# Two graph-attention and feed-forward layers on one core: the third attention's value stride, the experts' order on VectorE, and when the feed-forward stage loads its last rows

## Chip, cores and metric

The kernel runs as one program on one core of a Trainium2 chip. Its engines are TensorE (PE in the profile; PEld is its weight load), VectorE (DVE), ScalarE (ACT), GpSimd (POOL) and SyncE (SP), which here only issues DMAs. Each engine works through its own list of instructions in order, and waits on semaphores for the others.

The metric is the device time of one execution in microseconds. Before the change it is 2967.96 us (median of 3 runs, 2966.99 to 2968.54).

## What is computed

Input are 4096 rows `x` of 256 numbers and a 4096 x 4096 matrix `adj` of zeros and ones. Four blocks follow each other, each on the layer-normed result of the one before and added to it:

```python
x = x + L0_gnn(layernorm(x), adj)       # one graph attention, 4 heads of 64
x = x + L0_ffn(layernorm(x))            # 30 steps of a small recurrence
x = x + L1_gnn(layernorm(x), adj)       # two graph attentions, one after the other
x = x + L1_ffn(layernorm(x))            # a mixture of 6 experts, the best 2 for each row

# a graph attention, for each head:
h = x @ W;  f1 = h @ a1;  f2 = h @ a2
e = leaky_relu(f1[:, None] + f2[None, :], 0.2);  e = where(adj > 0, e, -9e15)
out = elu(softmax(e) @ h)

# a step of L0_ffn:
h = h + 0.01 * tanh(h);  h = h * sigmoid(h);  h = layernorm(h, ln_w, ln_b);  h = h @ W + b

# L1_ffn:
p = softmax(relu(f @ router_w1 + b1) @ router_w2 + b2);  top_w, top_i = top_k(p, 2)
r = softmax(top_w)
h1 = relu(f @ expert_w1 + b1);  h2 = relu(h1 @ expert_w2 + b2);  o = h2 @ expert_w3 + b3
y = sum over the two chosen experts of r * o
```

## The kernel before

The 4096 rows are 32 tiles of 128 rows (`NT`), or 8 groups of four tiles (`NG`, `G`). Intermediate rows go through tensors in device memory: `x1d` after the first attention, `x2d` after the feed-forward, `h1d` and `x3d` after the second and third attention. A ring of four row groups (`ring`, `load_ahead`) stays in SBUF all the time and is shared by all stages.

**Attention** (`attention`, called three times: tags g0, g1, g2). A front (L394 to L439) loads the row groups, turns them on TensorE, multiplies them with the weights, and makes for each tile and head the values `vals`: fp16, two parts of 2 x 65 numbers (upper and lower half of the number, and a column for the denominator). Then the main loop goes through 4 chunks of 8 tiles, 4 heads, and 8 steps of four tiles each (`units`, 128 in all). In a unit ScalarE and VectorE make the signs `st` (L464, L462), VectorE ands and xors them with the mask of edges (L569, L575), and TensorE does 64 matmuls (L521): an fp8 mask tile as weights, 130 columns of `vals` moving, accumulated in PSUM over all 32 source tiles. A head's sums are closed (`close`) by small VectorE and ScalarE operations between the next units. VectorE and ScalarE keep the written order in the main loop (`manual_schedule`); elsewhere a scheduler orders what engines and queues do.

The two numbers `apart` set how far the two parts of `vals` stand from each other in SBUF, in fp16 elements, and how far the two accumulators stand from each other in PSUM, in fp32 elements. The layers have (130, 130), (160, 130) and (130, 256): 260, 320 and 260 bytes for the values. The third layer has no layer norm ahead of it (`norm` is False); there, the sum over all rows that the front ends with goes through `xsb` (L431), a copy by GpSimd that spreads a column over 128 columns, which then are TensorE's weights in L435.

**Feed-forward** (L827 to L966). 30 steps for each of 8 row groups are 240 units; `slot(at)` is one turn of a pipeline over them, and holds pieces of six units: TensorE's turns of the rows `z` (L869, unit at-3), VectorE's `y` out of PSUM (L877, at-5), ScalarE's silu `z` and its fp16 half (L893, L897, at-2), VectorE's `lower` half (L898), a transposing DMA on SP (L902), ScalarE's tanh `th` (L907, unit at), GpSimd's sum of it (L908), VectorE's statistics (L917), ScalarE's `zT` (L924), GpSimd's power for the deviation (L928), and TensorE's product (L937, L940, at-4). PSUM holds two products `po`, so a unit's product waits for the `y` of the unit two before it. GpSimd's sum is made to follow `lower` by `follows`.

The stage's rows are the first attention's result, normed in place: `measure` (VectorE), `rate` (ScalarE and three GpSimd operations), `init` (ScalarE, or VectorE where `apart` is True). What is left of this when the attention ends is spread over the first slots by the table `opening`. The last step of the recurrence adds the same rows again. `slot` loads them a second time at slots 32, 56, ... 200 of the program's order (`load` for groups 0 to 3 into the ring, `load_apart` for the others); as SP is left to the scheduler, these eight loads can be issued as soon as their buffers are free.

**Experts** (from L1021). The rows are two halves of 2048 (`NTH` tiles and `NGH` groups each). `route(h)` norms a half, turns it (L1122), multiplies it with the router's weights (L1101, L1131), finds the best two experts of each row, and builds the list of rows by expert: `source` (which row is gathered into a place), `dest` (where its result goes), `expert` (which expert a tile of 128 places belongs to), `bsel` (that expert's biases), `ws` (the two weights). `route(0)` runs ahead, with the experts' weights `ew` loaded after its first four steps; `route(1)` is taken step by step in the loop over 74 tiles (`gather`, `turn`, `fetch`, `hidden`, `result`), where `fetch` reads the expert's number into registers. Each half's rows come through the ring, and ScalarE writes them, less one, to `acc`, to which `combine` adds the experts' results.

Of the kernel before, what the change touches and what calls it, by code (L numbers as in the profile page):

```python
# [23 lines left out]
P = 128  # L24
# [22 lines left out]
def gnn_ffn_kernel(ctx: ExitStack, tc: tile.TileContext, a: dict, out: bass.AP):  # L47
# [34 lines left out]
    def rows_of(t, g):  # L82
        return t[g * GR : (g + 1) * GR, :].rearrange("(r p) c -> p r c", p=P)
# [6 lines left out]
    def load_ahead(src, g, view=rows_of, queue=nc.sync):  # L90
        t = ring[:, turns[0] % 4]
        turns[0] += 1
        queue.dma_start(t, view(src, g))
        ahead[g] = t

    def over_std(pool, src):

        st = pool.tile([P, G, 6], F32, name="ln_st")
        mv = pool.tile([P, G, 2], F32, name="ln_mv")
        for r in range(G):  # L100
            nc.vector.bn_stats(st[:, r, :], src[:, r, :])  # L101
        for r in range(G):
            nc.vector.bn_aggr(mv[:, r, :], st[:, r, :])
        rstd = pool.tile([P, G], F32, name="ln_rstd")
        nc.vector.tensor_scalar(rstd, mv[:, :, 1], EPS, None, op0=OP.add)
        nc.gpsimd.tensor_tensor(rstd, rstd, mhalf, OP.pow)
        return rstd, mv
# [53 lines left out]
    def attention(tag, src, norm, w, front, chunks, first, ends, following, side={}, apart=(2 * DV, 2 * DV)):  # L161
# [7 lines left out]
        with ExitStack() as scope:  # L169
# [68 lines left out]
            with ExitStack() as ps:  # L238
# [189 lines left out]
                if sums is None:  # L428
                    xt = prep.tile([P, KC], F32, name="xt")
                    nc.vector.tensor_reduce(xt, xs, axis=AX.X, op=OP.add)  # L430
                    xsb = prep.tile([P, KC, P], F32, name="xsb")  # L431
                    nc.gpsimd.tensor_copy(xsb, xt[:, :, None].to_broadcast([P, KC, P]))
                    pt = small_ps()
                    for k in range(KC):
                        nc.tensor.matmul(pt[:, :C], xsb[:, k, :], w[:, k, :C], start=(k == 0), stop=(k == KC - 1))  # L435
                nc.scalar.activation(
# [304 lines left out]

    def load(g, queue=nc.sync):
        if g not in ahead:
            load_ahead(x1d, g, queue=queue)
        x1[g] = ahead.pop(g)

    def measure(g):
# [79 lines left out]
    with ExitStack() as scope:  # L827
# [7 lines left out]
        def load_apart(src, g):  # L835
            x1[g] = hold.tile([P, G, C], F32, name="x1")
            nc.sync.dma_start(x1[g], rows_of(src, g))

        for g in range(4, NG):
# [5 lines left out]

        th, zs, mvs, rs, zT, zT16, pos = {}, {}, {}, {}, {}, {}, {}
        units = FFN_STEPS * NG
        opening = {
            0: [(init, 2)],
            1: [(rate, 4), (rate, 5), (init, 3, True)],  # L850
            2: [(init, 4, True)],
            3: [(init, 5, True), (measure, 6)],
            4: [(rate, 6), (measure, 7)],
            5: [(init, 6), (rate, 7)],
            6: [(init, 7)],
        }
        def slot(at):
            g, part = divmod(at - 4 * NG, 3 * NG)
            if 0 <= g < NG and part == 0:
                if g < NG // 2:  # L860
                    load(g)
                else:
                    load_apart(x1d, g)
            u = at - 3
# [26 lines left out]
            if 0 <= u < units:  # L891
                z = zs[u] = work.tile([P, G, C], F32, name="z")
                ins = nc.scalar.activation(z, th.pop(u), AF.Silu, scale=0.01)  # L893
                if not u:
                    follows(ins, closed[1], "one change of tables")
                z16 = work.tile([P, 2, G, P], F16, name="z16", bufs=4)
                nc.scalar.activation(z16[:, 0], z[:, :, P:], AF.Identity, scale=scale[:, :1])  # L897
                lower = nc.vector.scalar_tensor_tensor(  # L898
                    z16[:, 1], z[:, :, P:], scale[:, :1], z16[:, 0], op0=OP.mult, op1=OP.subtract
                )  # L900
                zT16[u] = work.tile([P, 2 * G, P], F16, name="zT16", bufs=4)
                nc.sync.dma_start_transpose(zT16[u], z16.rearrange("p s r c -> p (s r c)"))  # L902
# [97 lines left out]
    for n in range(2):  # L1000
        attention(
            f"g{n + 1}",
            h1d if n else x2d,
            not n,
            layers[n + 1][0],
            None if n else centre_weights,
            [8, 8, 8, 8],
            False,
            to_rows(x3d, x2d) if n else to_rows(h1d),
            [NG // 2, x3d, runs_of] if n else [2, h1d],  # L1010
            {} if n else side,
            (2 * DV, 256) if n else (160, 2 * DV),
        )
# [7 lines left out]
    with ExitStack() as scope:  # L1021
# [3 lines left out]
        bT = one.tile([P, NB], F32, name="bT")  # L1025
        acc = one.tile([P, NT, C], F32, name="acc")
        ws = one.tile([P, 2, NT], F32, name="ws")
        bsel = [one.tile([P, T, 2 * KC], F32, name=f"bsel{h}") for h in range(2)]
        expert = [one.tile([P, T], I32, name=f"expert{h}") for h in range(2)]
        dest = [one.tile([P, T], I32, name=f"dest{h}") for h in range(2)]  # L1030
        source = [one.tile([P, T], I32, name=f"source{h}") for h in range(2)]
        ew = [one.tile([P, E, KC, C], F32, name=f"ew{i}") for i in range(3)]
        b3 = one.tile([P, E, C], F32, name="b3")
# [43 lines left out]
        def over(t, n=NTH, m=E):  # L1077
            return t[:, :, None].to_broadcast([P, n, m])

        def route(h, turned, bank):  # L1080

# [3 lines left out]
            def load(g):  # L1085
                if h * NGH + g not in ahead:
                    load_ahead(x3d, h * NGH + g, runs_of)
                rows[g] = ahead.pop(h * NGH + g)

            load(0)  # L1090
            load(1)
            for g in range(NGH + 2):
                if g + 2 < NGH:
                    load(g + 2)
                if g < NGH:
                    stds[g] = over_std(rwork, rows[g])
# [8 lines left out]
                if 1 <= g <= NGH:  # L1105
# [18 lines left out]
                    nc.scalar.activation(acc[:, at : at + G, :], t, AF.Identity, bias=mone)  # L1124
                    yield
                if 2 <= g:
                    u = g - 2
# [91 lines left out]
            for i in range(2):  # L1219
# [18 lines left out]
                yield  # L1238
            seen = rone.tile([P, T, E - 1], F32, name="seen")
            nc.vector.tensor_tensor(  # L1240
                seen,
                along[:, :T, None].to_broadcast([P, T, E - 1]),
                first[:, None, 1:].to_broadcast([P, T, E - 1]),
                OP.is_ge,
            )
            ex = rone.tile([P, T], F32, name="ex")
            nc.vector.tensor_reduce(ex, seen, axis=AX.X, op=OP.add)
            nc.vector.tensor_copy(expert[h], ex)
            lst = rone.tile([P, T, 2], F32, name="lst")
# [10 lines left out]
            nc.vector.tensor_copy(dest[h], df)  # L1260
            yield
            ohe = rone.tile([P, T, E], F32, name="ohe")
            nc.vector.tensor_tensor(
# [19 lines left out]
        with tc.tile_pool(name="r_ps", bufs=1, space=PSUM) as psum, tc.tile_pool(  # L1283
# [7 lines left out]
            nc.tensor.transpose(ps[:, :NB], br, ident[:NB, :NB])  # L1291
            nc.vector.tensor_copy(bT, ps[:, :NB])
            steps = route(0, turned, bank)
            for _ in range(4):
                next(steps)
            for i in range(3):
# [3 lines left out]
            nc.sync.dma_start(b3, bcast_rows(a["L1_ffn_expert_b3"]))  # L1300
            for _ in steps:
                pass

# [167 lines left out]
```

## Time and profile before

The profiled execution took 2983.79 us by its own time; its span from first to last instruction is 2982.0 us, at a mean granted TensorE clock of 0.98.

| stage | from, to (us) | PE | DVE | ACT | POOL | granted clock | DMA share |
|---|---|---|---|---|---|---|---|
| first attention | 0 to 603 | 548 | 567 | 536 | 40 | 0.98 | 0.76 |
| feed-forward | 603 to 1568 | 947 | 959 | 832 | 911 | 0.99 | 0.37 |
| second attention | 1568 to 2109 | 523 | 500 | 489 | 18 | 1.00 | 0.20 |
| third attention | 2109 to 2647 | 517 | 496 | 491 | 24 | 0.99 | 0.23 |
| experts | 2647 to 2982 | 260 | 216 | 115 | 167 | 0.90 | 0.40 |

The engine columns are busy microseconds within the stage. A stage's limit is read from which engine has no idle time there, and then from what the others wait for. TensorE's matmuls are pipelined and their ends are modelled, so its busy time says that it is always fed, not how fast it is; its speed is read from the number of matmuls in a stretch of time. The clock column matters because TensorE runs at half speed where the granted clock is 0.5.

Three stretches between stages have TensorE idle: 597 to 660 (busy 45 of 63 us), 2109 to 2166 (41 of 57 us) and 2647 to 2704 (23 of 57 us).

### The profile page before, as it was taken

How to read it: one execution, taken by the hardware profiler on the slowest of the kernel's cores; microseconds unless marked ns; L12 is line 12 of the kernel's file. 1: busy time of each engine (PE TensorE's matmuls, PEld its weight loads, DVE VectorE, ACT ScalarE, POOL GpSimd, SP SyncE). 2: the span in 40 equal slices, each digit the busy share in tenths (PEclk: the TensorE clock that was granted, in tenths of full speed). 3: DMA queues.
4: the chain of work that ended last, by engine and by line, in shares of the span. 5: the costliest groups of instructions: out<-in, count | busy, mean ns of one | idle time of the engine just before them, and what ended most of it. 6: DMA issues, size and time to landing. Idle time of an engine off the chain costs nothing. (4 is left out here: it accounts for less than half of the span.)

```text
span 2982.0 us, 82665 instructions
## 1 busy us (share of the span) xinstructions
PE 2795.9 (94%) x33923; PEld 2553.5 (86%) x33923; DVE 2737.1 (92%) x5769; ACT 2463.9 (83%) x3125; POOL 1159.1 (39%) x1084
## 2 busy tenths in 40 slices
PE   7899999979999999999998999999899999977986
PEld 5799999968888888888887999999799999967885
DVE  7999999999999999999998899999889999976665
ACT  5799999978888888888877999999799999954332
POOL 3000000079999999999982000000300000015563
PEclk9999999989999999999999999999999999988998
DMA  9999885043333333333353032120302222142243
GB/s 281 274 258 242 230 234 159 25 126 69 68 69 68 68 67 70 68 67 70 68 110 119 26 99 72 49 87 27 108 27 94 66 94 94 31 141 93 79 165 133
DMA packets 484450, 320.07 MB, mean 107 GB/s; under 512 B 416589, under 2 KB 445418, under 8 KB 477930
## 3 DMA queue, kind: packets, MB, share of 16 engines
q1 hardware_dynamic: 474034, 290.27, 36.1%
q0 software_dynamic: 7104, 19.41, 2.1%
q8 instruction: 268, 4.39, 0.6%
q10 hardware_dynamic: 2936, 5.11, 0.5%
q14 instruction: 108, 0.88, 0.1%
HBM read 183.00 MB, written 52.04 MB: 79 GB/s over the span
## 5 line engine op out<-in xcount | busy, mean ns | idle before, releaser
L521 PE MATMUL acc<-vals,st 128*128 128x130 f16 x12288 | 1425.1, 219 | 39.0 <-DVE u L476 30.6
L521 PE MATMUL acc<-vals,below 128*128 128x130 f16 x12288 | 1424.7, 221 | 14.0 <-DVE below L575 13.2
L464 ACT ACTIVATE st<-f1b,nf 128x1024 int8<-128x1024 f32 x1265 | 1334.2, 1145 | 30.3 <-PE acc L521 19.8
L521 PEld LDWEIGHTS <-below 128*128 128x128 fp8e4 x12288 | 1185.9, 97 | 55.0 <-issue 42.6
L521 PEld LDWEIGHTS <-st 128*128 128x128 fp8e4 x12288 | 1207.2, 98 | 9.6 <-DVE st L569 7.8
L937 PE MATMUL po<-wT,zT 128*128 128x256 f32 x1920 | 576.2, 382 | 6.1 <-DVE y L877 3.5
L940 PE MATMUL po<-w,zT 128*128 128x256 f16 x3840 | 577.9, 273 | 0.5 <-DMA zT<-z 0.5
L908 POOL TENSOR_TENSOR th<-th,y 128x1024 f32<-128x1024 f32 x232 | 548.9, 2366 | 14.5 <-DVE z_st L917 0.4
L940 PEld LDWEIGHTS <-zT 128*128 128x128 f16 x3840 | 376.6, 98 | 161.7 <-DMA zT<-z 1.2
L575 DVE TENSOR_TENSOR below<-m,st 128x1024 int32<-128x1024 int32 x384 | 469.9, 1224 | 32.6 <-DVE st L569 0.9
L569 DVE TENSOR_TENSOR st<-st,m 128x1024 int32<-128x1024 int32 x384 | 466.8, 1216 | 0.2
L877 DVE SCALAR_TENSOR_TENSOR y<-po,z_rs,bias 128x256 f32<-128x256 f32 x928 | 384.3, 476 | 2.2 <-PE tp L869 0.7
L917 DVE BATCH_NORM_STATS2 z_st<-z 128x6 f32<-128x256 f32 x960 | 335.5, 412 | 0.0
L937 PEld LDWEIGHTS po<-wT,zT 128*128 128x128 f32 x1920 | 291.1, 192 | 15.6 <-issue 3.7
L893 ACT ACTIVATE z<-th 128x1024 f32<-128x1024 f32 x240 | 251.9, 1050 | 17.6 <-POOL th L908 16.8
L928 POOL TENSOR_TENSOR z_rs<-z_rs,mhalf 128x4 f32<-128x4 f32 x240 | 245.4, 1022 | 3.1 <-ACT z_rs L927 3.1
L907 ACT ACTIVATE th<-y 128x1024 f32<-128x1024 f32 x232 | 241.7, 1042 | 0.0
L924 ACT COPY zT<-tp 128x512 f32<-128x512 f32 x240 | 140.4, 585 | 90.6 <-PE tp L869 89.5
L462 DVE TENSOR_SCALAR st<-f1b,nf 128x1024 int8<-128x1024 f32 x271 | 201.0, 742 | 6.2 <-PE acc L521 6.2
L760 POOL TENSOR_TENSOR x_rs<-x_rs,mhalf 128x4 f32<-128x4 f32 x8 | 9.4, 1175 | 505.3 <-ACT x_rs L759 505.3
L1046 POOL IOTA along_i<- 128x512 int32 (+1 forms) x5 | 2.8, 557 | 485.8 <-PE acc L521 485.7
L439 POOL MEMSET hs<- 128x4 f32 x3 | 0.3, 103 | 485.9 <-DVE u L493 485.9
(263 smaller groups left out, 3158.5 us busy)
## 6 DMA issues: line engine op xcount, KB each, us to landing
ring<-in_adj_dram SPq DMA_DIRECT2D x64, 1024.0 KB
m<-edges SPq DMA_DIRECT2D x32, 1024.0 KB
f1b<-fd SPq DMA_DIRECT2D x48, 512.0 KB
edges<-m SPq DMA_DIRECT2D x16, 1024.0 KB
y<-yd SPq DMA_DIRECT2D x16, 512.0 KB
ew<-in_L_ffn_expert_w_dram SPq DMA_DIRECT2D x18, 256.0 KB
t<-in_x_dram SPq DMA_DIRECT2D x8, 512.0 KB
old<-in_x_dram SPq DMA_DIRECT2D x16, 256.0 KB
```

The costliest lines, as they stand in the source:

```text
L464: nc.scalar.activation(out, f1, AF.Sign, bias=f2, scale=-1.0)
L521: nc.tensor.matmul(acc[:, i, part * apart_s : part * apart_s + 2 * DV], masked[part][:, at_i // TR, s, rows], values[:, j, h, part], start ...
L569: nc.vector.tensor_tensor(above, above, whole, OP.bitwise_and)
L575: nc.vector.tensor_tensor(below, whole, above, OP.bitwise_xor)
L877: nc.vector.scalar_tensor_tensor(t[:, r, :] if end else y[:, g * G + r, :], po[:, r, :], rstd[:, r : r + 1], t[:, r, :] if end else bias, ...
L893: ins = nc.scalar.activation(z, th.pop(u), AF.Silu, scale=0.01)
L907: nc.scalar.activation(th[at], was, AF.Tanh, scale=0.01)
L908: ins = (nc.gpsimd if at else nc.vector).tensor_tensor(th[at], th[at], was, OP.add)
L917: nc.vector.bn_stats(st[:, r, :], z[:, r, :])
L928: nc.gpsimd.tensor_tensor(rs[u], rs[u], mhalf, OP.pow)
L937: nc.tensor.matmul(po[:, r, :], src[:, r * P : (r + 1) * P], wT, start=True, stop=False)
L940: nc.tensor.matmul(po[:, r, :], src16[:, part * G + r, :], w16[:, other, :], start=False, stop=(part == 1 and other == 1),)
```

## The change

- The third attention's `apart` becomes the second's: values 160 elements (320 bytes) apart, accumulators 130. `vals` takes 15,360 bytes more of each partition.
- `xsb` goes; TensorE reads the column itself, repeated.
- Feed-forward: groups 4 and 5 are normed by ScalarE in slots 3 and 4, no longer by VectorE in slots 2 and 3; their rates come in slot 0, group 3 stays on VectorE. The eight second loads follow `lower` of the slot before them, so SP issues them at slots 32, 56, ... 200. `load` no longer looks for rows that are already there.
- Experts: the first half's `route` keeps the written order on VectorE. In it, the list's `source` and `dest` come ahead of `seen`, `ex`, `expert`, `ohe` and `bsel`. The second half's rows go straight to their place in `acc`, and no longer through the ring; its first two groups are loaded ahead of `route(0)` and measured within it (`measure_other`). The tiles of the pool are placed in another order.

By the engines' orders in the built program: on SP the eight row loads move from among the first feed-forward transposes to one after every 24th; the third layer's four first mask loads come ahead of most of its row loads; two loads of `x3d` come ahead of the experts' weights. On GpSimd the rates of groups 4 and 5 come ahead of the second `th`, and the first `ln_rstd` of the experts' front comes behind all the index tables. On ScalarE the norming of groups 4 to 7 stands in four slots that follow each other. On TensorE eight turns and two router products of the second half come ahead of the first gathered rows.

```diff
@@ attention, end of the front
-                    xsb = prep.tile([P, KC, P], F32, name="xsb")
-                    nc.gpsimd.tensor_copy(xsb, xt[:, :, None].to_broadcast([P, KC, P]))
                     pt = small_ps()
                     for k in range(KC):
-                        nc.tensor.matmul(pt[:, :C], xsb[:, k, :], w[:, k, :C], start=(k == 0), stop=(k == KC - 1))
+                        nc.tensor.matmul(
+                            pt[:, :C], xt[:, k : k + 1].to_broadcast([P, P]), w[:, k, :C], start=(k == 0), stop=(k == KC - 1)
+                        )
@@ feed-forward
         opening = {
-            0: [(init, 2)],
-            1: [(rate, 4), (rate, 5), (init, 3, True)],
-            2: [(init, 4, True)],
-            3: [(init, 5, True), (measure, 6)],
-            4: [(rate, 6), (measure, 7)],
-            5: [(init, 6), (rate, 7)],
+            0: [(init, 2), (rate, 4), (rate, 5)],
+            1: [(init, 3, True)],
+            3: [(init, 4), (measure, 6)],
+            4: [(rate, 6), (init, 5), (measure, 7)],
+            5: [(rate, 7), (init, 6)],
             6: [(init, 7)],
         }
         def slot(at):
             g, part = divmod(at - 4 * NG, 3 * NG)
             if 0 <= g < NG and part == 0:
-                if g < NG // 2:
-                    load(g)
-                else:
-                    load_apart(x1d, g)
+                ins = load(g) if g < NG // 2 else load_apart(x1d, g)
+                follows(ins, halved[0], "in mid-stage, when the queue has room")
...
+                halved[:] = [lower]
@@ the second and third attention
-            (2 * DV, 256) if n else (160, 2 * DV),
+            (160, 2 * DV),
@@ experts
-        acc = one.tile([P, NT, C], F32, name="acc")
-        ws = one.tile([P, 2, NT], F32, name="ws")
...
-        ew = [one.tile([P, E, KC, C], F32, name=f"ew{i}") for i in range(3)]
+        ew = [one.tile([P, E, KC, C], F32, name=f"ew{i}") for i in (2, 1, 0)][::-1]
+        acc = one.tile([P, NT, C], F32, name="acc")
+        ws = one.tile([P, 2, NT], F32, name="ws")
...
+        early = {}
+
+        def rest(g):
+            return acc[:, (NGH + g) * G : (NGH + g + 1) * G, :]
+
+        def measure_other(g):
+            early[g] = over_std(rone, rest(g), f"_{g}")
...
             def load(g):
-                if h * NGH + g not in ahead:
-                    load_ahead(x3d, h * NGH + g, runs_of)
-                rows[g] = ahead.pop(h * NGH + g)
+                if h:
+                    rows[g] = rest(g)
+                    if g in early:
+                        stds[g] = early.pop(g)
+                    else:
+                        nc.sync.dma_start(rows[g], runs_of(x3d, NGH + g))
+                else:
+                    rows[g] = ahead.pop(g)
...
-                if g < NGH:
+                if g < NGH and g not in stds:
                     stds[g] = over_std(rwork, rows[g])
...
+                if not h and g >= NGH:
+                    measure_other(g - NGH)
...
+            for g in range(2):
+                nc.sync.dma_start(rest(g), runs_of(x3d, NGH + g))
             steps = route(0, turned, bank)
-            for _ in range(4):
-                next(steps)
+            with tc.manual_schedule(engines={mybir.EngineType.DVE}):
+                for _ in range(4):
+                    next(steps)
...
-            for _ in steps:
-                pass
+            with tc.manual_schedule(engines={mybir.EngineType.DVE}):
+                for _ in steps:
+                    pass
```

## The prediction

> **What bounds the kernel now.** I read the page first, then the busy time by stage in windows, then the waits of TensorE in those windows, then the timelines at the three places that the diff touches.
>
> ```profile
> PE 2795.9 (94%) x33923; PEld 2553.5 (86%) x33923; DVE 2737.1 (92%) x5769; ACT 2463.9 (83%) x3125; POOL 1159.1 (39%) x1084
> ```
>
> TensorE is nearly always busy, and VectorE nearly as much; an average over five stages doesn't say which one ends last. So I take the two later attention layers side by side, first all engines, then TensorE on L521 alone (columns: window and its length; PE busy and count, weight loads, then in the first pair VectorE, ScalarE, GpSimd; granted clock, DMA share, GB/s).
>
> ```profile
> 1700.00:1800.00 100.00, 98.97 (x1741) 98.57 (x1739) 94.91 (x109) 96.26 (x98) 0.00 (x0) 1.00 0.25 78
> 2300.00:2400.00 100.00, 99.25 (x1714) 98.76 (x1712) 95.02 (x107) 95.11 (x97) 0.00 (x0) 1.00 0.26 81
> ```
> ```profile
> 1640.00:1760.00 120.00, 118.59 (x2084) 118.09 (x2082) 1.00 0.19 61
> 1760.00:1880.00 120.00, 118.66 (x2085) 118.12 (x2082) 1.00 0.23 72
> 2300.00:2420.00 120.00, 118.94 (x2053) 118.33 (x2051) 1.00 0.26 81
> 2420.00:2540.00 120.00, 118.79 (x2053) 118.30 (x2051) 1.00 0.25 81
> ```
>
> Both layers are bound by TensorE: it is 99% busy at clock 1.00, VectorE and ScalarE near 95%. Yet the second layer (stride 320 bytes) gets 2084 matmuls through in 120 us, the third (260 bytes) 2053.
>
> The feed-forward stage runs at TensorE's pace too: between 660 and 1530 us no wait of TensorE is recorded at all, and a unit takes nine groups of 0.4355 us, 3.92 us, against 3.80 us of VectorE. So it costs whatever delays the start of that unbroken run:
>
> ```profile
> 617.39 1.22 PE L937 MATMUL po<-wT,zT 128*128 128x256 f32 x2 [1.05 <-ACT zT L924]
> 631.79 0.67 PE L937 MATMUL po<-wT,zT 128*128 128x256 f32 x2 [3.47 <-DVE y L877]
> 638.15 0.70 PE L937 MATMUL po<-wT,zT 128*128 128x256 f32 x2 [0.53 <-ACT zT L924]
> 643.43 0.70 PE L937 MATMUL po<-wT,zT 128*128 128x256 f32 x2 [1.09 <-ACT zT L924]
> ```
> ```profile
> 617.05 3.37 DVE L779 TENSOR_SCALAR x<-x,x_rs,x_nm 128x256 f32<-128x256 f32 x4
> 622.60 2.10 DVE L779 TENSOR_SCALAR x<-x,x_rs,x_nm 128x256 f32<-128x256 f32 x4
> ```
> ```profile
> 619.99 1.06 ACT L893 ACTIVATE z<-th 128x1024 f32<-128x1024 f32 x1 [2.45 <-POOL th L908]
> ```
>
> These are the starts of units 0, 2, 3 and 4. Unit 2 waits for VectorE's first y, which stands behind the two L779 blocks; ScalarE waits 2.45 us for GpSimd, which does the rates of groups 4 and 5 between two th.
>
> The experts' stage has the third stretch in which TensorE is idle:
>
> ```profile
> 2654.24 1.48 POOL L106 TENSOR_TENSOR ln_rstd<-ln_rstd,mhalf 128x4 f32<-128x4 f32 x1
> ```
> ```profile
> 2675.61 0.18 DVE L1134 TENSOR_TENSOR lg<-ps_l,g_w 128x24 f32<-128x24 f32 x1 [3.48 <-PE ps_l L1131]
> 2697.09 0.17 DVE L1259 TENSOR_SCALAR source<-sf 128x37 int32<-128x37 f32 x1
> ```
> ```profile
> 2698.15 1.54 POOL L1315 DMA_INDIRECT gx<-nd,source  x1 [0.26 <-DVE ln_mv L103]
> ```
>
> From the last logits to the row list, 21.4 us, VectorE works through one chain; then the first gather goes, and expert matmuls start at 2704.33. From there to 2957 TensorE's recorded waits sum to 16.6 us.
>
> **Stride of 320 bytes.** The third layer gets exactly the second's (160, 130) for values and accumulators. Its 8192 matmuls at 120/2053 us take 478.8 us, at 120/2084.5 us 471.6 us: **-7.2 us**, short pauses at a head's change included. In unbroken stretches of 3 us starts lie 57.64 ns apart in the third layer and 56.61 ns in the second: 8192 x 1.03 = 8.4 us, the upper end. Lower end 6: the third layer has a longer last step per head (L627, 0.69 us, where the second has L625, 0.42). Is it the values' stride or the accumulator's 256? The first layer has (130, 130) and 57.64 ns in the same stretches, so the accumulator's is worth nothing. The Trainium skill (SBUF — State Buffer, the note on cachelines under "Door 1: The DMA port swizzle") gives lines of 16 bytes and a penalty for each change of line; a row of 260 bytes touches 17 lines whether it starts on a multiple of 320 or of 260, so by that rule the gain is nil. The row decides: 7.2, not 0. Writing the values costs nothing more: L380 takes 1.08 us and L385 1.23 us in both layers.
>
> **The copy xsb.** One GpSimd copy (1.33 us at 2150.66) goes; its reader L435 starts at 2159.53 after a wait for ScalarE's rt (L349), so 0. A broadcast column as weights already stands in L341. The masks' four loads (1 MB each) come earlier, because the layout now equals the second layer's; TensorE waits for no DMA there, and the stretch ends with VectorE, busy without a gap from 2134 to 2165: 0, between -1 and +1.
>
> **Feed-forward's start.** Groups 4 and 5 go from VectorE to ScalarE: VectorE loses 3.30 + 2.03 = 5.3 us, ScalarE gains 2 x 1.98 (the block at 632.71 is one). The rates of 4 and 5 go ahead of th 1, into GpSimd's idle 8.79 us before 611.58. Eight row loads leave this stretch's queue. Followed through: th 2 is added from 615.5 (lower, L898, ends 615.46) to 617.95 instead of 619.9; ScalarE has done init 4 at 619.4 and z 2 at 620.5. VectorE reaches the measuring of group 6 at 619.3, where its rows, loaded at 616.97 with group 7's, land by about 621 (an estimate: 512 KB took 2 us of transfer at 608 to 610); it ends at 622.6, the next measuring at 626.5, the first y at 628.05. Unit 2 starts at about 628.3. Now ScalarE is late next: four slots of 3.33 + 1.98 us put zT of unit 3 at 633.6 and of unit 4 at 638.9, against 638.15 and 643.43. **-4.3 us** at unit 4. From there on the run is unbroken as before.
>
> The Trainium skill (TensorE: Matmul & The Clock Gate, part 1) halves the clock after some 3.4 us of idling. The trace shows it: after the 3.47 us gap four groups take 0.85 us instead of 0.43 (632.7 to 636.1). My gaps are 1.0, 1.4 and 1.8 us, so by the rule no halving; if the clock did fall it costs 1.7 us once. Ends: -1.5 (ScalarE's four slots late, and one halving) and -6.
>
> **Loads in mid-stage.** Eight loads of 512 KB on SP, each waiting for the lower half of the unit before. That is the wait of the transpose issued just ahead of it, so it adds none; behind it stands the next transpose. At 1002.32 a lower half is done, its transpose moves at 1003 to 1005, and TensorE reads it at 1008.5: 3.5 us to spare, and DMA is idle two thirds of the time. A load of 2 us fits in: 0. The nearest row is the stage's end, where four stores of 512 KB go between transposes from 1542 on and TensorE waits for none.
>
> **Experts' front.** The list's chain loses ws, seen, ex, expert, ohe, sel, bsel and two weight copies, some 4.0 us before source, and gains four n (1.33 us): about -2.7. The gather also loses the ln_rstd ahead of it (0.9). Against it: the first ln_rstd now stands behind all of GpSimd's index work, 2.3 us later, so n 0 starts 1.5 us later, and n 3 waits for the second group's logits, which TensorE's own order mostly hides: lg 1.7 us later. Net -1.9 at the gather. Bias and weights, now made after source, end near the first xT (2700.5), so the first expert matmul moves by -2.3. Some transposes and two L1101 matmuls (2.3 us) of the other half move into TensorE's idle time ahead of the loop; half of that I do not count, as the loop is not all TensorE's. The new loads of x3d need rows that have long been stored; the weights behind them come 2.7 us later, and 10 us before use. **-3.0**, between +1 and -4.6.
>
> **Sum.** -7.2 - 4.3 - 3.0 = -14.5 us on a profiled execution of 2983.79 (its span is 2982.0). The runs shown have a median of 2967.96, so **2953.5**.
>
> **Rivals.**
> 1. *VectorE or ScalarE takes over in the third layer*, at 95% now; the stride gives 0: -7.3, **2960.7**. For it: they would rise to 96%. Against: the second layer runs at that pace with the same loads.
> 2. *ScalarE holds the feed-forward's start and the fixed order holds the experts'*: these give +0 and +1, leaving the stride: **2961.8**. For it: eight more ScalarE operations in four slots, and n 3 behind a logit. Against: ScalarE waited 2.45, 2.92 and 2.76 us there.
> 3. *Slower: the loads hold up transposes.* One load ahead of a transpose in SP's queue delays it by its transfer; beyond 3.5 us TensorE stops. At the 67 GB/s which that stage moves on average 512 KB take 7.8 us: 4.3 x 8 = 34 us, **2987**. It outweighs the gains from 1.8 us per load. Against it: the stores at the stage's end.
> 4. *A change that doesn't take*: nothing speaks for it; the instruction order moves as told.
>
> **Numbers.** Forecast 0.72, rival 1 0.09, rival 2 0.11, rival 3 0.04, all else 0.04. The forecast's own range, from the ends above: 2947 to 2958; rivals 1 and 2 take it to **2946 to 2961**. What can be told from no change is 0.2%, 5.9 us: faster 0.92, within 0.04, slower 0.04.
>
> **What would show it.** 2084 matmuls per 120 us in the third layer; unit 4 of the feed-forward 4 us earlier after the attention's end; no TensorE wait for zT near the eight loads; source some 19 us after the last logits, expert matmuls 2 us earlier relative to the attention's end. Wrong it is if the third layer keeps 2053, if gaps of TensorE appear every 24 units in the feed-forward, or if the last logits come over 4 us later.

## The result, and the profile after

| | median (us) | runs | ratio to before |
|---|---|---|---|
| before | 2967.01 | 2965.2 to 2968.54, 6 runs | |
| changed | 2954.56 | 2947.02 to 2955.54, 6 runs | 0.9953, 95% interval 0.9943 to 0.9963 |

The change saves 12.5 us; 14.5 were forecast. The profiled execution of the changed kernel took 2954.59 us, its span is 2952.9.

The busy times of the engines hardly differ:

```profile
PE 2792.2 (95%) x33923; PEld 2550.2 (86%) x33923; DVE 2735.9 (93%) x5761; ACT 2467.6 (84%) x3133; POOL 1160.4 (39%) x1083
```

In windows of the third layer, TensorE on L521 alone (window, length, busy and count, granted clock, DMA share, GB/s), the count that was 2053 is now the second layer's:

```profile
2300.00:2420.00 120.00, 118.86 (x2085) 1.00 0.26 81
2420.00:2540.00 120.00, 118.85 (x2084) 1.00 0.27 85
```

TensorE's timeline at the start of the feed-forward (start, duration, instruction, and in brackets the idle time ahead of it and who ended it): units 2, 3 and 4 of the changed kernel, whose attention ends 1.7 us earlier than in the profile before, at 601.5.

```profile
626.52 0.70 PE L936 MATMUL po<-wT,zT 128*128 128x256 f32 x2
...
632.64 0.70 PE L936 MATMUL po<-wT,zT 128*128 128x256 f32 x2 [1.51 <-ACT zT L923]
...
637.92 0.70 PE L936 MATMUL po<-wT,zT 128*128 128x256 f32 x2 [1.09 <-ACT zT L923]
```

The 3.47 us wait for y ahead of unit 2 is gone; from unit 4 on no wait of TensorE is recorded, up to the stage's end at 1562 us.

VectorE's timeline in the experts' front, from the last logits to the row list and beyond:

```profile
2664.75 0.18 DVE L1148 TENSOR_TENSOR lg<-ps_l,g_w 128x24 f32<-128x24 f32 x1 [0.40 <-PE ps_l L1145]
...
2684.11 0.15 DVE L1263 TENSOR_SCALAR source<-sf 128x37 int32<-128x37 f32 x1
2684.26 0.34 DVE L1267 TENSOR_TENSOR seen<-along,first 128x185 f32<-128x185 f32 x1
...
2687.97 1.07 DVE L1287 TENSOR_REDUCE bsel<-sel 128x148 f32<-128x888 f32 x1
2688.95 0.17 DVE L1290 TENSOR_TENSOR ws<-top,top 128x16 f32<-128x16 f32 x1
```

In the profile before, the same three stood ahead of source, which came at 2697.09:

```profile
2679.79 0.17 DVE L1276 TENSOR_TENSOR ws<-top,top 128x16 f32<-128x16 f32 x1
...
2683.93 0.34 DVE L1240 TENSOR_TENSOR seen<-along,first 128x185 f32<-128x185 f32 x1
...
2687.19 1.07 DVE L1273 TENSOR_REDUCE bsel<-sel 128x148 f32<-128x888 f32 x1
```

Now they follow it: 19.4 us from lg to source in place of 21.5.

**Where the time went, by stage.** The table divides each trace at TensorE's own marks: last product and first product of each stage. "Changed (2)" and "before (2)" are second profiles, from the experiments below.

| from, to (us) | before | before (2) | changed | changed (2) |
|---|---|---|---|---|
| last matmul of first attention, last of feed-forward | 964.8 | 964.8 | 960.9 | 961.1 |
| to the first L521 of the second layer | 60.2 | 60.2 | 60.4 | 60.2 |
| second layer's L521, first to last | 480.9 | 481.4 | 481.1 | 481.3 |
| third layer's front | 52.4 | 53.3 | 53.9 | 53.1 |
| third layer's L521, first to last | 485.1 | 486.5 | 479.0 | 479.5 |
| to the first expert matmul | 58.1 | 58.3 | 54.8 | 54.1 |
| expert loop | 249.7 | 252.8 | 232.8 | 247.1 |
| from there to the end | 28.1 | 27.8 | 28.8 | 28.0 |
| start to last matmul of first attention | 602.9 | 603.9 | 601.2 | 599.5 |

Three stretches have moved as the forecast said: the feed-forward 3.8 us, the third layer some 5 us (front and L521 together), the way to the first expert matmul 3.3 to 4.2 us. The last row is no part of the change: in the 13 profiles of this document that leave the first attention as it was, it lies between 597 and 605 us. One more row, the expert loop, moved by 17 us between the first two profiles that could be compared, and nobody had forecast that. The profiled execution of before (2983.8 us) lies 16 us above the median of its runs, so the loop had to be looked at before anything else.

### The profile page after: what moved, and what is told of

Same layout as the page of the kernel before. It is cut to its first block, busy times and chain, and to the rows that moved or that the text cites. A ratio compares the mean times of both kernels' runs of the same rounds, so it can differ in the third digit from the quotient of the medians.

```text
span 2952.9 us, 82649 instructions
## 1 busy us (share of the span) xinstructions
PE 2792.2 (95%) x33923; PEld 2550.2 (86%) x33923; DVE 2735.9 (93%) x5761; ACT 2467.6 (84%) x3133; POOL 1160.4 (39%) x1083
## 5 line engine op out<-in xcount | busy, mean ns | idle before, releaser
L521 PE MATMUL acc<-vals,st 128*128 128x130 f16 x12288 | 1417.8, 220 | 39.0 <-DVE u L476 30.6
L521 PE MATMUL acc<-vals,below 128*128 128x130 f16 x12288 | 1417.4, 221 | 13.2 <-DVE below L575 12.3
L521 PEld LDWEIGHTS <-below 128*128 128x128 fp8e4 x12288 | 1195.8, 97 | 55.0 <-issue 48.0
L521 PEld LDWEIGHTS <-st 128*128 128x128 fp8e4 x12288 | 1206.7, 98 | 9.3 <-DVE st L569 7.5
L891 ACT ACTIVATE z<-th 128x1024 f32<-128x1024 f32 x240 | 251.7, 1049 | 15.0 <-POOL th L907 14.5
```

The costliest lines, as they stand in the source:

```text
L521: nc.tensor.matmul(acc[:, i, part * apart_s : part * apart_s + 2 * DV], masked[part][:, at_i // TR, s, rows], values[:, j, h, part], start ...
```

## The experiments

**1. A second profile of each kernel.** Edit: none.

> The kernel before, once more, for a second profile. In the profiled executions the experts' stage took 335.6 us before the change (from the last attention matmul to the end of the span) and 316.3 us after, 19.3 us less, where 3.0 were forecast; but the profiled execution of before, 2983.8 us, lies 16 us over the median of its runs. Theory A: that execution was an outlier whose extra 16 us lay in the experts' loop; this profile shows that stage at about 320 us and a time of 2967. Theory B: the stage really takes 335 us in the kernel before; then it does so here too, and the change gains 19 us there and loses 7 us somewhere that the profiles hide.

> The changed kernel once more, on the chip of this set of runs. The kernel before takes 2967 us on one chip and 2984 on another; in its profiles on the slower one the expert loop (first to last expert matmul) takes 249.7 and 252.8 us, and in the one profile of the changed kernel, on the faster one, 232.8. Theory A: that is the chip, and the change does nothing to the loop: if the kernel before is at 2980 or more here, the loop of the changed kernel takes 249 to 254 us, and the ratio is 0.995 to 0.9965 as before. Theory B: the change shortens the loop: 233 us here too, and a ratio of 0.99 on a slow chip.

Measured: the first set ran on a chip on which the kernel before takes 2983.68 us; the repeat took 2985.81 us (ratio 1.0007, 0.9998 to 1.0017), its loop 252.8 us. The changed kernel's repeat, on another chip (before: 2980.88), took 2965.65 us, ratio 0.9945 (0.9929 to 0.9962), its loop 247.1 us. Neither theory was right to the word: the profile before was no outlier (A's first half) and the change doesn't shorten the loop by 17 us (B). It goes with the chip: where before takes 2981 to 2984 us the loop took 245 to 254 us in every profile, changed or not; the last two kernels of experiment 5 ran on a chip where before takes 2967.6, and their loops took 231.7 us each. The ratio is the same on both kinds. Profiles of two kernels are to be compared stage by stage only where they come from one chip, or for stages that don't depend on it.

TensorE's idle time within the loop was 14.7 us in the repeat and 2.3 us in the first profile, which is most of the 14.3 us between them; in all profiles it was 13 to 21 us on the slower kind and 2 to 6 us on the other. The two largest waits of the repeat (releaser, total us, times, longest):

```profile
PE ph L1372 <- DVE h L1385: 8.3, 10, 1.3
PE ph L1372 <- ACT h L1383: 2.4, 3, 1.4
```

and all waits of the first profile:

```profile
PE ph L1372 <- DVE h L1385: 1.7, 3, 1.1
PE ps L1189 <- DVE below L1185: 0.6, 1, 0.6
```

Most tiles run alike on both kinds: VectorE's next h starts 1.31 us after the tile's turn. It starts over 1.6 us after it in 12 to 14 of the 72 to 74 tiles on the faster kind, and in 27 to 36 on the slower. Why is open.

**2. The stride alone.**

```diff
-                        nc.tensor.matmul(pt[:, :C], xsb[:, k, :], w[:, k, :C], ...)
+                        nc.tensor.matmul(pt[:, :C], xt[:, k : k + 1].to_broadcast([P, P]), w[:, k, :C], ...)
-            (2 * DV, 256) if n else (160, 2 * DV),
+            (160, 2 * DV),
```

> The kernel before with the third layer's stride of 320 bytes, and without the xsb copy, whose space the wider values need. Theory A: the main loop of the third layer takes 479 us in place of 485.3 (2084 matmuls in 120 us), and the layer's front, from the last matmul of the second layer to the first of the third, 53.9 us in place of 52.2, because the wider values move the masks in memory and with them the order of the work: together -4.6 us, 2962.4. Theory B: the front's 1.7 us come from elsewhere in the change; then the front stays at 52.2 and the time is 2960.7.

Measured: 2976.11 us against 2983.68, ratio 0.9979 (0.997 to 0.9989): between -3 and -9 us. L521 took 479.2 us, the front 53.9, as theory A has it. And one thing that A didn't have, worth 1.1 us: the first expert matmul comes 57.0 us after the last attention matmul, not 58.1, in a part of the kernel that this edit doesn't touch (see the experts' front below).

**3. What the spacing follows.** The stride alone, in the changed kernel: 264 bytes in the second layer and 272 in the third; and 288 in the third.

```diff
-            (160, 2 * DV),
+            (136, 2 * DV) if n else (132, 2 * DV),
```

> The changed kernel with a stride of 264 bytes in the second layer and of 272 in the third, to see what the spacing of the matmuls follows. By alignment to 8 bytes both are quick (2084 matmuls in 120 us), by alignment to 16 bytes the third alone, by alignment to 32 bytes or more neither (2053 in both, 7 us more in each of the two layers against 320 bytes).

> The changed kernel with a stride of 288 bytes in the third layer in place of 320; the smaller values leave the masks where they lay before the change, and the instruction order in the layer's front is that of the kernel before. Theory A: what makes a matmul quick is a stride that is a multiple of 32 bytes: 2084 matmuls in 120 us, and without the two L464 ahead of the front's hc no second pause over 2 us and no halved clock in the front, so 1 to 2.5 us less than the changed kernel on the same chip. Theory B: the stride has to be a multiple of 64: 2053 matmuls, 5 us more than the changed kernel.

Measured, in windows of the first of these kernels (columns as above; two of the second layer, one of the third):

```profile
1760.00:1880.00 120.00, 118.77 (x2054) 1.00 0.22 72
1880.00:2000.00 120.00, 118.78 (x2055) 1.00 0.21 68
...
2440.00:2560.00 120.00, 118.85 (x2084) 1.00 0.23 72
```

264 bytes is slow, 272 is quick, 288 and 320 too: a start on 16 bytes is what counts, not 32 or 64 (in the built programs vals itself begins on a multiple of 16). The second layer's L521 takes 487.7 us in place of 481.1, the third's 478.2. As the loss in the second layer eats up the gain in the third, that kernel gained little (2976.19, ratio 0.998, 0.997 to 0.9991).

288 bytes gave 2966.57, ratio 0.9946 (0.9929 to 0.9963) beside 0.9945 of the changed kernel on the same chip. Theory A's first half holds, its second doesn't: the front with the old order takes 53.1 us, and so does the changed kernel's this time. The long pause is gone (1.3 us at most), but the clock was half all the same, for 13.7 us at the loop's start.

**4. The feed-forward's part, whole and its loads alone.**

```diff
-            1: [(rate, 4), (rate, 5), (init, 3, True)],
-            2: [(init, 4, True)],
-            3: [(init, 5, True), (measure, 6)],
...
+            0: [(init, 2), (rate, 4), (rate, 5)],
+            1: [(init, 3, True)],
+            3: [(init, 4), (measure, 6)],
...
+                follows(ins, halved[0], "in mid-stage, when the queue has room")
```

> The kernel before with the feed-forward's part of the change alone: the new opening and the eight loads in mid-stage. Theory A: unit 4 of the stage starts 36.5 us after the attention's last matmul in place of 40.3, no later wait of TensorE in the stage, time 2963.1 (-3.9). Theory B: part of that is given back further on in the stage or at its end by the loads; the stage then ends less than 3 us earlier and the time is over 2964.5.

> The kernel before with its own opening of the feed-forward, but with the eight row loads put behind a lower half in mid-stage. Theory A: the loads are worth nothing by themselves, and all of the stage's gain is the opening's: 964.8 us from the last attention matmul to the last of the feed-forward, as before (961.0 with both). Theory B: the loads leaving the queue of the stage's start are what gives the gain: 961 to 962 us.

Measured: with both, 961.0 us from the attention's last matmul to the stage's last, -3.8; with `follows` alone and the old table, 964.8, as before. All of the gain is the opening's, and the loads neither cost nor bring anything in this stage. In whole times, 2981.74 us (ratio 0.9995, 0.9986 to 1.0005) and 2979.47 (0.9997, 0.9986 to 1.0007): 3.8 us are more than these runs can tell, and only the stage's marks in the trace show them: 964.8 us in each of the eight profiles with the old opening, 960.9 to 961.1 in five with the new one (961.7 in the sixth, that of experiment 6). The whole time of the first came out less than its stage gained: its third layer took 539.8 us (front and L521) where most profiles of the old layer show 537.5. It is the same 2.3 us as in the second profile of before: at that layer's start the trace shows half clock for 13.7 us in those two, and for 6.8 us in the others.

**5. The experts' part, whole and in pieces.** The whole part; then only the moved lines (seen, ex and what follows, behind source); then all without the move; then all without the fixed order:

```diff
-            for _ in steps:
-                pass
+            with tc.manual_schedule(engines={mybir.EngineType.DVE}):
+                for _ in steps:
+                    pass
```

> The kernel before with the experts' part of the change alone. Theory A: the forecast's step: first expert matmul 2 to 3 us earlier after the last attention matmul, the rest of the stage as in an ordinary execution of before: time 2963 to 2964.5 (-2.5 to -4). Theory B: the two groups measured and loaded ahead also shorten the expert loop itself, since its waits fell from 11.6 us to 1.7 us in the profiles: -8 us or more, under 2959.

> The kernel before, where only the experts' numbers and bias weights (seen, ex, expert, ohe, sel, bsel) are made behind the row list. Theory A: the forecast's chain term: source 2.1 us sooner after the last logits (19.4 in place of 21.5), and the first expert matmul 2 us earlier: nearly all of what the experts' part brings, the fixed order and the other half's two groups bringing under 1 us. Theory B: without the fixed order the scheduler puts other work of VectorE into the gap: source less than 1 us sooner.

> The experts' part of the change without the move of seen, ex and what follows them behind the row list: fixed order of VectorE's work and the other half's two groups alone. Moving those lines alone changed nothing (source 21.5 us after the last logits). Theory A: the fixed order is what takes work out of the list's chain (ws, ohe, sel and bsel), and the move is worth only seen and ex within it: source 19.8 to 20.4 us after the last logits, between the 19.4 of the whole part and the 21.5 of before. Theory B: both are needed: 21 us or more.

> The experts' part of the change without the fixed order: the move behind the row list and the other half's two groups, placed by the scheduler. Theory A: the scheduler leaves ws, seen, ex, ohe and bsel ahead of the list and puts four n of the other half ahead of it as well: source 22.5 to 23.5 us after the last logits, over 1 us later than before the change, and the first expert matmul up to 1 us later. Theory B: the order doesn't matter: 19.4 us as with the whole part.

| kernel | last lg to source (us) | last attention matmul to first expert matmul | time, ratio to before |
|---|---|---|---|
| before | 21.5 | 58.1 | |
| whole part | 19.4 | 55.3 | 2979.93, 0.9989 (0.9979 to 0.9999) |
| move alone | 21.5 | 58.2 | 2982.55, 1.0002 (0.9992 to 1.0013) |
| fixed order, no move | 20.7 | 58.7 | 2966.05, 0.9989 (0.9977 to 1.0) |
| move, no fixed order | 22.1 | 57.8 | 2963.1, 0.9986 (0.9975 to 0.9997) |

The last two stand beside a before of 2967.6 us, the others beside 2983.68 and 2981.17. VectorE's timeline of the move alone shows why it does nothing:

```profile
2677.13 0.17 DVE L1276 TENSOR_TENSOR ws<-top,top 128x16 f32<-128x16 f32 x1
...
2681.27 0.35 DVE L1253 TENSOR_TENSOR seen<-along,first 128x185 f32<-128x185 f32 x1
...
2684.52 1.07 DVE L1273 TENSOR_REDUCE bsel<-sel 128x148 f32<-128x888 f32 x1
...
2694.42 0.17 DVE L1249 TENSOR_SCALAR source<-sf 128x37 int32<-128x37 f32 x1
```

In the text seen (L1253) now stands behind source (L1249); on the engine it stands 13 us ahead of it, where it always was, since a scheduler puts it there as soon as its inputs are ready. The move takes effect only under a fixed order. The fixed order without the move brings source 0.8 us sooner (outside both theories' numbers), but the second gather then starts 2.2 us after the first (1.8 before, 1.5 with the whole part), and TensorE waits 5.3 us for gathered rows, so the first expert matmul gains nothing. Without the fixed order source comes 0.7 us later than before, less than the 1 us or more that theory A gave it, and the first expert matmul is not later but 0.3 us sooner. Of these kernels only the one with both brings the 2.8 us; all but the move alone have the other half's two groups as well, and what those bring by themselves was not tried. In whole times, the three kernels with the other half's two groups can't be told apart.

**6. The first layer on 16 bytes too.** It runs at 260 bytes and 57.65 ns. At 272 its values take 2.25 KB a partition more than there is, so one buffer of st is given for it.

```diff
-    ..., side={}, apart=(2 * DV, 2 * DV)):
+    ..., side={}, apart=(136, 2 * DV)):
-            spool = scope.enter_context(tc.tile_pool(name=f"{tag}_steps", bufs=4))
+            spool = scope.enter_context(tc.tile_pool(name=f"{tag}_steps", bufs=3 if first else 4))
```

> The changed kernel with a stride of 272 bytes in the first layer too (the second and third keep 320), paid for with 3 in place of 4 buffers for st in that layer. Theory A, spacing follows a 16-byte start and the first layer is bound by TensorE where no transfer holds it up: clean spacing 56.67 ns in place of 57.65 in the first layer, the attention's last matmul 3 to 8 us earlier, and a ratio to the kernel before 0.001 to 0.0027 lower than the changed kernel's 0.9945 to 0.9953. Theory B: the third st buffer holds ScalarE or VectorE up, or the first layer is bound by its transfers (DMA 0.85 busy until 460 us): no gain, or slower by some us.

Measured: 3004.35 us, ratio 1.0076 (1.0059 to 1.0093). TensorE's waits in that layer, from 100 us to its end, of this kernel

```profile
PE acc L521 <- DVE u L476: 38.3, 22, 3.8
PE acc L521 <- DVE below L575: 14.4, 23, 1.0
```

and of the changed kernel:

```profile
PE acc L521 <- DVE u L476: 19.8, 16, 3.0
PE acc L521 <- DVE below L575: 2.0, 7, 0.5
```

The spacing did fall to 56.7 ns, worth 8 us over 8192 matmuls, but the layer ends 36 us later: TensorE waits 31 us more for VectorE. Buffer and stride weren't tried apart: that the buffer is the cause is likely, not shown.

## Why the prediction was right, point by point

**Stride: -7.2 forecast, -5.3 measured at the layer.** The mechanism is as stated: 2084 matmuls per 120 us, and the accumulators' distance is worth nothing (288 and 272 bytes are quick with 130; 264 is slow with 130, and the old layer was with 256). In stretches without a pause the starts lie 56.67 ns apart in place of 57.65: 8192 x 0.98 = 8.0 us. The prediction's upper end, 8.4, rested on 56.61 from stretches of 3 us. Two things take some of it back: pauses, whose excess (after the first 25 us of the loop, over 0.08 us each) sums to 7.9 us in place of 7.0, and the clock, at half speed for 45 matmuls in place of 26 at the loop's start, 52 ns more each, 1.0 us. So L521 takes 479.0 in place of 485.1, -6.1. In the kernel with 272 bytes, where 28 matmuls ran at half clock, it took 478.2: -6.9, close to the forecast. The front took 53.1 to 53.9 us, against 52.3 to 53.3 in the eight profiles with the old layer; front and L521 together 532.8 (mean of four) against 538.1 (mean of eight): -5.3. What the term left out is what the clock and the front take back.

The prediction set the cacheline rule of the Trainium skill (SBUF — State Buffer) against the row of matmuls measured; the row was right on the amount. The rule has the right grain, 16 bytes; but the number of lines touched, 17 at every stride tried, is not the cost. Where a row begins is.

**The copy and the masks: 0 forecast, 0 to +1.5.** The copy's removal is not a gain but a condition: with xsb in place the wider values exceed SBUF by 160 bytes a partition. The forecast looked for waits for DMAs, and missed what loads that come earlier let the scheduler do. ScalarE's timeline in the front before and in the changed kernel's first profile, then TensorE's in the latter:

```profile
2133.23 2.23 ACT L380 ACTIVATE vals<-v 128x1040 f16<-128x1040 f32 x2 [1.36 <-POOL v L370]
2135.36 1.05 ACT L325 COPY hc<-ph 128x512 f32<-128x512 f32 x2
2138.00 1.13 ACT L464 ACTIVATE st<-f1b,nf 128x1024 int8<-128x1024 f32 x1
```
```profile
2126.99 1.15 ACT L464 ACTIVATE st<-f1b,nf 128x1024 int8<-128x1024 f32 x1 [0.28 <-DMA f1b<-fd]
2128.07 1.09 ACT L380 ACTIVATE vals<-v 128x1040 f16<-128x1040 f32 x1
2129.06 1.12 ACT L464 ACTIVATE st<-f1b,nf 128x1024 int8<-128x1024 f32 x1
2130.09 1.07 ACT L380 ACTIVATE vals<-v 128x1040 f16<-128x1040 f32 x1
2131.07 1.04 ACT L325 COPY hc<-ph 128x512 f32<-128x512 f32 x2
```
```profile
2131.68 5.51 PE L305 MATMUL ph<-g_w,xT 128*128 128x264 f32 x16 [2.14 <-ACT hc L325]
```

Two st for the main loop are now worked in ahead of the hc that TensorE waits for: it waits 2.14 us, where the longest such wait was 1.3, and its next 16 matmuls take 5.51 us in place of 3.83, at half clock. In the second profile the wait is there (2.2 us) and the half clock is not. With 288 bytes, where that order is as before, the whole time was no better. The front's own times, 53.1 to 53.9 us against 52.3 in most profiles before, put it at 1.5 us at most.

**Feed-forward's start: -4.3 forecast, -3.8 measured.** Unit 2 started 25.1 us after the attention's last matmul (forecast 25.2), unit 3 31.2 (30.5), unit 4 36.5 (35.8). By the prediction's own times unit 4 would have come 4.5 us sooner, not 4.3; it came 3.9 sooner. The 0.7 us are ScalarE's: the sum gave it four slots without a wait, and in one of them it waited 0.54 us for GpSimd's rate of group 6:

```profile
627.39 2.08 ACT L782 ACTIVATE x<-x,x_nm,x_rs 128x256 f32<-128x256 f32 x4 [0.54 <-POOL x_nm L763]
```

The loads cost nothing. The clock did not fall after the gaps of 1.5 and 1.1 us in this profile. The Trainium skill (TensorE: Matmul & The Clock Gate, part 1) has it fall after an idle window of some 3.4 us, and the prediction took that as a limit for a gap. As such it doesn't hold here. In the kernel of experiment 6 a gap of 1.51 us at the same place did halve the clock; the stage took 0.7 us longer there, part of which came before the gap. Of the eight profiles with the old opening, all with the wait for y ahead of unit 2, the clock fell after it in five; unit 4 started 40.3 us after the attention in all eight, so there it cost nothing. What decides is shown in the last section.

**Experts' front: -3.0 forecast, -2.8 alone and -3.3 to -4.2 in the changed kernel.** The -3.0 was -2.3 at the first expert matmul and some gain in the loop, from work moved ahead of it; of the latter nothing can be seen next to the chips (on one chip the loop took 252.8 us before and 253.5 with this part alone, and on another 232). At the first expert matmul the sum was near, and its terms weren't. In the part alone the chain gave -2.1 (forecast -2.7); the gather's -0.9 didn't come, as it goes 1.04 us after source where it went 1.06 after, so the ln_rstd ahead of it had not held it; and the logits did not come 1.7 us later but 0.3 us sooner. From source to the first expert matmul it gained 0.4 us more, as forecast. That the three errors nearly cancelled is luck.

The logits' term failed in two ways. In the part alone ln_rstd 0 does not move on GpSimd at all: it starts 8.0 us after the last attention matmul, as before. In the changed kernel it does stand behind the index work, but that work starts earlier: ln_rstd 0 comes at 4.7 us, and the last logits at 27.7 to 28.2 in place of 29.4. The first line of that work and ln_rstd 0, before and changed:

```profile
2646.52 0.17 POOL L1046 IOTA along_i<- 128x37 int32 x1 [485.67 <-PE acc L521]
...
2654.24 1.48 POOL L106 TENSOR_TENSOR ln_rstd<-ln_rstd,mhalf 128x4 f32<-128x4 f32 x1
```
```profile
2630.64 0.17 POOL L1045 IOTA along_i<- 128x37 int32 x1 [473.29 <-DVE below L575]
...
2641.30 1.04 POOL L106 TENSOR_TENSOR ln_rstd<-ln_rstd,mhalf 128x4 f32<-128x4 f32 x1 [1.84 <-DVE ln_rstd L105]
```

Before, the index work waited for the last attention matmul; now for a below of VectorE's, and begins 6 us ahead of the attention's end in place of just after it. It is the third layer's 320 bytes that do this: in the four profiles of kernels that have them it is so, and in none of the other ten, not even with 272 and 288 bytes, where the matmuls are as quick. The built programs say why. The pool of the index tiles begins at byte 157,248 of a partition and ends near 176,000. The signs st, which TensorE reads to the last, begin at 165,152 before, at 172,320 with 288 bytes, and at 180,512 with 320, behind the whole pool. So 1.1 us of the experts' front come with the size of the values (57.0 us in place of 58.1 with the stride alone). They are no part of what the 7.2 stood for.

**The sum.** 3.8 + 5.3 + 3.3 to 4.2 = 12.4 to 13.3 us from the stages, and 12.5 from the medians, whose interval is 11 to 17 us. Of the 2 us that the forecast had too much, the stride's term accounts for nearly all. The range was not the sum of its parts: the ends that the prediction gives add up to 2948 to 2962.5, not 2947 to 2958. The result lies in both.

**Rivals.** No engine took over in the third layer (2084, with VectorE and ScalarE at 95 to 96%), both openings, the feed-forward's and the experts', gained, and no transfer delayed a transpose: unit after unit ran on without a recorded wait.

## What to carry to other kernels

Where a long run of matmuls is bound by TensorE, let every row of the moving operand begin on a multiple of 16 bytes; here, for fp16 rows of 130, 12 bytes of padding to a row of 260 are worth 1.7% of the spacing. If a buffer has to be given for them, measure whether it pays: in the first layer it did not. Moving a line in the text can change nothing where a scheduler orders an engine, as here: fix the order, or look at the instruction order first. A tile whose size changes can move what is placed behind it, and with that the waits of work that has nothing to do with it; compare when each engine's first instruction of the next stage is released, and by whom.

## What the runs showed of the hardware

- Off the 16-byte grid the matmuls alternate. At 264 bytes, where the first part of each pair begins on 16 bytes and the second 8 bytes off, starts lie 55.8 ns after a first part and 59.4 after a second; at 260 bytes, where the second is 4 or 12 off and half of the first 8 off, 55.8 and 59.5; on the grid 56.7 and 56.7. So with every second row off the grid the loss is as large as with three in four.
- TensorE's clock changes only on a grid of 3.41 us. Within each of the 14 profiles all half-clock stretches begin on one grid (to 0.005 us), and except for the one at the program's end they last a multiple of its step. Where the grid lies differs from profile to profile.
- What decides is how busy TensorE was in the grid's last window. From the first L521 to the end of the third attention, over all profiles: after a window at full clock that was busy for up to 0.42 of its length, the clock was half in the next one, 69 times of 69. After 0.43 to 0.49 it was half 4 times of 43, above that never in 10,147. From half clock it came back after every window that was busy for 0.79 or more (87), and after none below 0.77 (112). The shares are the profile's, in which a matmul's end is modelled, and the limits are read off these kernels alone; in the experts' stage, with its small matmuls, 19 of some 1,350 windows don't follow them. Two windows in a row around the wait for y ahead of unit 2, from the profile before and from the move alone, which has the same code there (window, length, busy and count, granted clock, DMA share, GB/s):

```profile
629.34:632.75 3.41, 0.96 (x7) 1.00 0.50 167
632.75:636.16 3.41, 3.41 (x15) 0.50 0.36 78
```
```profile
626.82:630.24 3.42, 1.50 (x10) 1.00 0.57 163
630.24:633.65 3.41, 2.88 (x21) 1.00 0.58 89
```

  The waits are alike (3.5 and 3.1 us, ended at the same point of the stage), and the grid cuts them differently: TensorE is busy for 0.28 of the first window, or for 0.44. So too in the third layer's front, where the windows with the waits of 2.14 and 2.2 us were 0.41 and 0.47 busy, and at that layer's start, where the same code had 6.8 or 13.7 us of half clock, 2.3 us of time.
- The same kernel takes 2967 us on some chips and 2981 to 2984 on others; where stages can be compared, the difference lies in the expert loop (232 us against 245 to 254), whose tiles depend on each other across engines, and not in the stages that TensorE's rate sets (the second layer's L521 at 320 bytes takes 480.7 to 481.8 us on both). Three chips are told apart in the experiments, one fast and two slow; that it is the chip itself and nothing else about those runs is likely, not shown.
